# Latent attention on one NeuronCore: the low half of a split as a subtraction on VectorE, with a batch's side work in another order

## The chip, the cores and the metric

The kernel runs on one core of a Trainium2 chip. The metric is the device time of one execution in microseconds (us). Below, PE is TensorE's matmul, PEld its weight load, DVE is VectorE, ACT is ScalarE, POOL is GpSimd, and SP is SyncE, which issues most DMAs. L362 means line 362 of the kernel.

## The reference, cut to what matters

The input is 8 batches of 1024 tokens of width 256, all float32. A first stage is latent attention with 16 heads of 16 and one rotary part of 32 shared by all heads; a second stage is two layers of windowed attention with an MLP. The change is in the first stage only:

```python
xn = layernorm(x)
c_kv = xn @ W_kv_down                     # 256 -> 128
k_rope = rotary(c_kv @ W_k_rope);  q_rope = rotary(xn @ W_q_rope)
k = c_kv @ W_k_up;  v = c_kv @ W_v_up;  q = xn @ W_q      # 16 heads of 16
scores = (q . k per head + q_rope . k_rope) / sqrt(16 + 32), causal
x = x + softmax(scores) @ v @ W_o
...                                       # then two layers of the second stage
```

## The kernel before, in words

**Units and steps.** In `mla` the scores of a batch are cut into 36 units, each one a set of key blocks and queries that fills 512 columns for four heads. The loop `for step in range(len(units) ...)` runs one unit a step, 36 steps a batch, 8 batches, and then an epilogue that finishes the last units. The order of the instructions on PE, DVE, ACT and POOL is the written order (`manual_schedule`). A step s does, in this order:

- `scores` of unit s: 16-head products of `k` and `q` on PE (L461) into two tiles of two PSUM banks each, and two exponentials on ACT, 128x1024 each, into `pt` (L469). `pt` has six buffers, that is three units.
- `turned` of unit s-1: each of the two `pt` tiles is multiplied on DVE by `er`, the exponential of the rotary scores (L483). After the first of the two, `settle` runs what is owed on DVE from the step before (the output's add L576, and the rotary factors L342 and L349).
- `values` of unit s-2: products of `pt` and `v` on PE into `acc` (L496). When a group of heads is complete, `ended` copies `acc` on ACT.
- the side work that the table lists for the step, first what is not named `low`, then `low`.
- what has come due after `ended`: `inverse` three steps later (a reciprocal on DVE, L528, and the DMAs through `zr` that spread it; for the last pair of a batch also the verdict on the sums, L1846, L1847, L1840), and `scaled` seven steps later (a multiplication on DVE, L562).

**Side work.** The table before the loop holds (step, who, name, arguments). `who` is the batch relative to the one whose scores run: -1 is the batch before, 1 the next, 2 the one after it. Each batch needs all of this once:

- `load`, `statistics` (DVE), `normalise` (ACT), `turn` (four transposes on PE, a copy on ACT): x, normalised and transposed, as `xnT`.
- `down`, `value`, `rope_q`, `rope_k`: products on PE (all through `times`, L201, as four column tiles side by side), with a copy on ACT or a multiplication on DVE.
- `query` m, n, c: half c of the product for the q of eight heads and 512 tokens; `keys` m, n: the product for k. With the last half `halves` copies the sum from PSUM to `t[:, 0]` on ACT, rounded to the type float32r.
- `low`: the rest, sum minus rounded sum, which makes `t[:, 1]`. Before, PE adds the product of `minus` (minus the identity) and `t[:, 0]` onto the sum in PSUM (L362), and ACT copies the result. Then `place_q` or `place_k` issues two DMAs on SP that lay both halves out for `scores`. There are eight of these a batch.
- `rotary` c, kb: rotary scores of a key block on PE, 512 columns or fewer at the diagonal, and their exponential into `er` on ACT (L424), at the diagonal also a mask on POOL.
- `squares` (ACT) and `reach` (PE, and a maximum on DVE, L443): a check on the size of the rotary vectors.
- `out_add` t, i: half i of an output product on PE; after the second an add on DVE (L576) and a store to DRAM.

All single-bank products share a pool of two PSUM banks: a bank is free again when its last reader is through. For the batches before the first, the same table runs ahead of the loop (who 1 and 2 only). In the last batch, from the step `ALONE` on, which is one past the last step with who 0, the two banks become a third tile for `scores`. The second stage's first weights and tables are loaded when the memory of the first stage's side work is free, near the end of the last batch.

Of the kernel before, what the change touches and what calls it, by code (L numbers as in the profile page):

```python
# [30 lines left out]
F32R = mybir.dt.float32r  # L31
AF = mybir.ActivationFunctionType
ALU = mybir.AluOpType
# [3 lines left out]
P = 128  # L37
# [45 lines left out]
def preln_mla_local_kernel(  # L83
# [27 lines left out]
    nc = tc.nc  # L111
    B = x.shape[0]
# [4 lines left out]
    ident = const.tile([P, P], F32, name="ident")  # L117
# [38 lines left out]
    def mla(ctx: ExitStack, verdict):  # L156


        wp = ctx.enter_context(tc.tile_pool(name="w_mla", bufs=1))
# [23 lines left out]
        on_v, on_a = Evacuate(nc, "v"), Evacuate(nc, "a")  # L183
# [55 lines left out]
                    lo = (a if same else 1 - a) * HR  # L239
                    nc.scalar.copy(dst[:, :, n * DR + a * HR : n * DR + a * HR + HR], src[:, :, lo : lo + HR])  # L240

        minus = wp.tile([P, P], F32R, name="minus")
        nc.scalar.mul(minus, ident, -1.0)

        vs = []
        for i in range(2):
            t = of[i].tile([P, NT, NH * VW + 32 - VW], F32, name=f"v{i}")
# [15 lines left out]
        def settle():  # L263
            while owed:
                owed.pop(0)()

        class Batch:
# [91 lines left out]

            def low(self):  # L360
                ps, t, then, args = self.pending
                nc.tensor.matmul(ps, minus, t[:, 0], start=False, stop=True, skip_group_check=True)  # L362
                on_a(t[:, 1], ps)
                then(t.bitcast(F32), *args)

            def query(self, m, n, c, part=None):
# [218 lines left out]
        def at(step, who, name, *args):  # L585
            beside.setdefault(step, []).append((who, name, args))

        for step, who, *what in (
            (0, -1, "out_add", 4, 0), (0, 0, "query", 1, 1, 0), (0, 0, "squares", 0),
            (1, -1, "out_add", 4, 1), (1, 0, "query", 1, 1, 1),  # L590
            (2, -1, "out_add", 6, 0), (2, 0, "low"),
            (3, -1, "out_add", 6, 1), (3, 0, "squares", 1),
            (4, 0, "value", 2), (4, 0, "rotary", 1, 3),
            (5, 0, "rotary", 1, 4), (5, 0, "rotary", 1, 5),
            (6, 0, "rotary", 1, 6), (6, 0, "reach"),
            (7, 0, "rotary", 0, 0),
            (8, 0, "keys", 1, 0), (8, 1, "normalise", 0, 0),
            (9, 0, "query", 0, 0, 0), (9, 0, "low"),
            (10, 0, "query", 0, 0, 1),
            (11, 0, "low"), (11, 1, "normalise", 0, 1), (11, 1, "normalise", 0, 2), (11, 1, "statistics", 1, 0),  # L600
            (12, 0, "query", 1, 0, 0), (12, 0, "query", 1, 0, 1), (12, 1, "normalise", 0, 3),
            (13, -1, "out_add", 0, 0), (13, 0, "low"), (13, 1, "statistics", 1, 1),
            (14, -1, "out_add", 0, 1), (14, 0, "keys", 1, 1),
            (15, -1, "out_add", 2, 0), (15, 0, "low"),
            (16, -1, "out_add", 2, 1), (16, 1, "normalise", 1, 0), (16, 1, "normalise", 1, 1),
            (17, 0, "rotary", 0, 2), (17, 1, "turn", 0, 0),
            (18, 1, "turn", 0, 1),
            (19, 1, "down", 0, 0), (19, 1, "normalise", 1, 2),
            (20, 1, "down", 0, 1), (20, 2, "load"), (20, 1, "normalise", 1, 3),
            (21, 1, "turn", 1, 0), (21, 1, "turn", 1, 1),  # L610
            (22, 1, "keys", 0, 0),
            (23, 0, "rotary", 0, 1), (23, 1, "low"),
            (24, 1, "down", 1, 0), (24, 0, "rotary", 0, 3),
            (25, 1, "down", 1, 1),
            (26, 1, "value", 0), (26, 2, "statistics", 0, 0),
            (27, 1, "rope_k", 0), (27, 1, "value", 1),
            (28, 1, "rope_q", 0, 0), (28, 1, "rope_q", 0, 1),
            (29, 1, "query", 0, 1, 0), (29, 1, "query", 0, 1, 1),
            (30, 1, "low"),
            (31, 1, "value", 3), (31, 2, "statistics", 0, 1),  # L620
            (32, 1, "rope_q", 1, 0), (32, 1, "rope_q", 1, 1), (32, 1, "keys", 0, 1),
            (33, 1, "rope_k", 1), (33, 1, "low"),
            (34, 1, "rotary", 1, 0), (34, 1, "rotary", 1, 1),
            (35, 1, "rotary", 1, 2), (35, 1, "rotary", 1, 7),
        ):
            at(step, who, *what)

# [2 lines left out]
        def do(b, step, low=False):  # L630
            for who, name, args in beside.get(step, []):
                if (name == "low") == low and 0 <= b + who < B:
                    act = getattr(batches[b + who], name)

                    if b == B - 1 and who == 0 and name.startswith("out"):
                        held.append((act, args))
                    else:
                        act(*args)


        units = []
# [15 lines left out]
        line, due = [], []  # L657
        with tc.manual_schedule(engines={E.PE, E.DVE, E.Activation, E.Pool}):
            for b in range(B + 1):
                for step in range(len(units) if b < B else 17):  # L660
                    if b == B - 1 and step == ALONE:
                        banks.close()
                        third = banks.enter_context(tc.tile_pool(name="pscore2", bufs=1, space=PSUM))
                        shared = itertools.cycle((pscore, pscore, third))
                    if b < B:
                        if step == 0:
                            batches[b].start()
                        line.append((batches[b], units[step], batches[b].scores(step, units[step])))
                    if len(line) > 1 or b == B:
                        for bt, unit, pts in line[-2 : -1] if b < B else line[-1:] if step == 0 else []:  # L670
                            bt.turned(unit, pts)
                    if b == B and step == 0:
                        for act, args in held[:2]:
                            act(*args)
                    ended = []
                    if len(line) > 2 or b == B and line:
                        bt, unit, pts = line.pop(0)
                        ended = [(bt, e) for e in bt.values(unit, pts)]
                    if b == B and step == 0:
                        for act, args in held[2:]:  # L680
                            act(*args)
                    if b == B:
                        settle()
                    do(b, step)
                    do(b, step, low=True)
                    if b == B:
                        settle()
                    for what in due:
                        what[0] -= 1
                    while due and due[0][0] == 0:  # L690
                        due.pop(0)[1]()
                    for bt, (c, g) in ended:
                        if (bt.b, c) == (B - 1, 0):
                            bt.straight(g)
                        elif g % 2:
                            due.append([3, lambda bt=bt, c=c, g=g: bt.inverse(c, g // 2)])
                            due.append([7, lambda bt=bt, c=c, g=g: bt.scaled(c, g // 2)])
                            due.sort(key=lambda what: what[0])
# [1152 lines left out]
    with ExitStack() as one:  # L1851
        mla(one, verdict)
# [9 lines left out]
    with tc.tile_pool(name="psum_v", bufs=1, space=PSUM) as psum:  # L1862
        ps = psum.tile([1, 1], F32, name="psbad")
# [80 lines left out]
```

## Time and profile before

| what | us |
|---|---|
| median of 3 runs (lowest to highest) | 3214.92 (3214.23 to 3216.42) |
| the profiled execution | 3218.66 |
| its span, first to last instruction | 3216.7 |
| DVE L483, two a unit, x576 | 678.7 busy, 1221 ns each |
| ACT L469, two a unit, x576 | 559.3 busy, 1028 ns each |
| PE L496 and L461, x3072 each | 314.9 and 252.7 busy |

Busy time is the union of an engine's instructions; the mean of one is longer than the distance between two that are queued, since they overlap. Matmuls are pipelined and their ends are modelled, so PE's busy share says little alone. An answer on waits lists who waited for whom, the total, the times and the longest. The mean granted TensorE clock is 0.992 of full speed, and it is 1.00 in every middle batch of the first stage.

### The profile page before, as it was taken

To read this page: it belongs to the slowest core of one execution; us is meant where nothing else is said; L and a number is where in the kernel's file an instruction comes from. 1 tells how busy PE (TensorE), PEld (TensorE's weight loads), DVE (VectorE), ACT (ScalarE), POOL (GpSimd) and SP (SyncE) were. 2 spreads that over 40 slices of the span, in tenths; PEclk is the share of its full clock that TensorE was granted. 3 is DMA by queue.
4 is the path that set the end of the run, shared out by engine and by line. 5 is a ranking of instruction groups with operands and counts; after the bars stand their busy time and mean duration, and the time that the engine had idled before them with its cause. 6 is when DMAs were issued, how large, how long until landed. Compare 5 with 4: busy or idle time off the path is not lost.

```text
span 3216.7 us, 112643 instructions
## 1 busy us (share of the span) xinstructions
PE 3139.2 (98%) x50082; PEld 1453.9 (45%) x50082; DVE 2589.3 (80%) x3784; ACT 1738.6 (54%) x2179; POOL 1359.5 (42%) x1065
## 2 busy tenths in 40 slices
PE   8999999999877999999999999999999999999998
PEld 2443444444323444444445444444544445454454
DVE  5898989898869888787888877787877788787773
ACT  6999899988722444444444443444444443444441
POOL 1111110110047655555565554655555555554540
PEclk9999999999998999999999999999999999999999
DMA  4334333423444354454545445454544545454431
GB/s 120 82 88 116 74 99 91 119 70 85 121 128 116 92 145 113 126 132 109 130 120 146 115 121 159 113 146 133 149 125 126 138 123 135 134 149 117 119 108 55
DMA packets 411613, 376.99 MB, mean 117 GB/s; under 512 B 174655, under 2 KB 353262, under 8 KB 410990
## 3 DMA queue, kind: packets, MB, share of 16 engines
q1 hardware_dynamic: 409134, 367.29, 43.2%
q8 instruction: 395, 6.47, 0.9%
q10 hardware_dynamic: 1984, 2.41, 0.2%
q14 instruction: 100, 0.82, 0.1%
HBM read 173.82 MB, written 141.00 MB: 98 GB/s over the span
## 4 chain that ended last, share of the span: by engine, by line
PE 90%; DVE 3%; DMA 2%; ACT 1%; issue 1%; SPq 1%; POOL 0%; DVEq 0%; ACTq 0%; POOLq 0%
PE ag L722 19%; PE pair L722 13%; PE psy L722 10%; PE acc L496 8%; PE psw L722 7%; PE sc L461 6%; PE pv L722 6%; PE o L1055 6%; PE pair L1014 5%; PE psR L201 2%; PE psq L201 2%; PE s L1063 2%; PE psx L201 2%; ACT pt L469 1%; PE psc L201 1%
## 5 line engine op out<-in xcount | busy, mean ns | idle before, releaser
L483 DVE TENSOR_TENSOR pt<-pt,er 128x1024 f32<-128x1024 f32 x576 | 678.7, 1221 | 62.9 <-ACT pt L469 62.5
L958 POOL TENSOR_TENSOR t<-t,t 128x1024 f32<-128x1024 f32 x128 | 304.4, 2378 | 801.9 <-DVE t L954 801.9
L722 PE MATMUL ag<-d,l 128*32 128x512 f32 x5632 | 639.7, 593 | 1.2 <-DVE xs L1095 0.6
L469 ACT ACTIVATE pt<-sc 128x1024 f32<-128x1024 f32 x576 | 559.3, 1028 | 54.7 <-PE sc L461 39.3
L1020 ACT ACTIVATE pt<-pair 128x1024 f32<-128x1024 f32 (+1 forms) x256 | 235.2, 968 | 538.1 <-PE pair L1014 503.2
L722 PE MATMUL pair<-l_qkv,xT 128*32 128x512 f32 x4096 | 474.0, 599 | 3.8 <-DMA xT<-zx 2.6
L126 POOL TENSOR_TENSOR rn<-ss,half 128x16 f32<-128x16 f32 x128 | 373.2, 2916 | 13.7
L722 PEld LDWEIGHTS ag<-d,l 128*32 128x32 f32 x5632 | 177.6, 110 | 373.6 <-issue 354.9
L496 PE MATMUL acc<-pt,v 128*32 128x512 f32 (+3 forms) x3072 | 314.9, 496 | 10.4 <-DVE pt L483 10.2
L949 ACT ACTIVATE sq<-pair 128x1024 f32<-128x1024 f32 x128 | 131.2, 1025 | 350.4 <-issue 311.4
L722 PE MATMUL psy<-l,hid 128*32 128x256 f32 x5120 | 282.1, 379 | 0.0
L426 POOL TENSOR_SCALAR_AFFINE_SELECT er<-er 128x128 f32<-128x128 f32 x64 | 49.1, 771 | 532.0 <-ACT er L424 532.0
L722 PEld LDWEIGHTS pair<-l_qkv,xT 128*32 128x32 f32 x4096 | 132.0, 111 | 306.6 <-issue 284.0
L461 PE MATMUL sc<-q,k 32*128 32x512 f32 (+3 forms) x3072 | 252.7, 381 | 7.5 <-ACT pt L469 6.6
L951 DVE TENSOR_TENSOR t<-pair,l_cos 128x1024 f32<-128x1024 f32 x128 | 156.1, 1219 | 121.3 <-ACT sq L949 121.1
L964 POOL TENSOR_TENSOR t<-t,rn 128x1024 f32<-128x1024 f32 x128 | 243.7, 1904 | 10.0
L722 PE MATMUL pv<-l_qkv,xT 128*32 128x512 f32 x2048 | 247.3, 592 | 0.0
L1055 PEld LDWEIGHTS o<-pt,v 128*32 128x32 f32 x7680 | 215.3, 110 | 68.0 <-issue 51.9
L1187 DVE SCALAR_TENSOR_TENSOR hid<-ag,l_b,ge 128x512 f32<-128x512 f32 x160 | 116.8, 730 | 157.7 <-ACT ge L1186 86.5
L1055 PE MATMUL o<-pt,v 128*32 128x128 f32 x7680 | 234.8, 273 | 3.1 <-POOL pt L1022 2.8
L722 PE MATMUL psw<-l_o,oT 128*32 128x256 f32 x4096 | 237.0, 383 | 0.4 <-DVE xs L1224 0.4
L1073 DVE RECIPROCAL rs<-s 128x256 f32<-128x256 f32 x128 | 223.2, 1743 | 15.6 <-PE s L1063 15.5
(331 smaller groups left out, 4480.2 us busy)
## 6 DMA issues: line engine op xcount, KB each, us to landing
z<-turned SPq DMA_DIRECT2D x512, 128.0 KB
qkT<-z SPq DMA_DIRECT2D x128, 512.0 KB
y<-xs SPq DMA_DIRECT2D x128, 128.0 KB
h<-y SPq DMA_DIRECT2D x32, 512.0 KB
zx<-turneds SPq DMA_DIRECT2D x120, 128.0 KB
xT<-zx SPq DMA_DIRECT2D x240, 64.0 KB
zh<-turnedh SPq DMA_DIRECT2D x120, 128.0 KB
d<-zh SPq DMA_DIRECT2D x30, 512.0 KB
```

The lines of the kernel that those rows point to most:

```text
L126: nc.gpsimd.tensor_tensor(out_, in_, half[:, :n], ALU.pow)
L201: nc.tensor.matmul(out[four], w[:, four], rhs, start=start, stop=stop)
L461: nc.tensor.matmul(two[n // 2][:, n % 2, lo : lo + w], k[rows], q[rows, h], start=(h == 1), stop=(h == 0),)
L469: nc.scalar.activation(pt, sc, AF.Exp, scale=SCALE)
L483: nc.vector.tensor_tensor(t, t, er.to_broadcast([P, 1024 // w, w]), ALU.mult)
L496: nc.tensor.matmul(self.acc[g][32 * n : 32 * n + 32, q0 - c * 512 :], self.v[:, kb, h * VW - at : h * VW - at + 32], pts[n // 2][:, n % 2, ...
L722: nc.tensor.matmul(out[four], w[:, four], rhs, start=start, stop=stop)
L958: nc.gpsimd.tensor_tensor(t1, t1, t2, ALU.add)
L964: nc.gpsimd.tensor_tensor(t1, t1, rn.unsqueeze(3).to_broadcast([P, 2, HEADS, DH]), ALU.mult)
L1020: nc.scalar.activation(pt[:, :, : n * P], flat[:, :, : n * P], AF.Exp, scale=-1.0)
L1055: nc.tensor.matmul(o[32 * j : 32 * j + 32, g, a, :], vs[m][:, h * DH + a * 32 : h * DH + a * 32 + 32], pts[m][g][:, place(j), off : off + ...
L1073: nc.vector.reciprocal(rs, s)
```

## The change

`minus` goes. `low` subtracts on DVE: the sum is read from PSUM, `t[:, 0]` from SBUF, and `t[:, 1]` is written. ACT no longer copies a second time. The table holds the same 74 entries in other steps, some for another batch (for example `query` 1 1 and `squares` 0 now run a batch ahead, and `value` 3 in place of `value` 2 is the one that runs late). The epilogue has 15 steps in place of 17, since the last `out_add` stands in step 14.

```diff
--- before.py
+++ after.py
@@ -239,9 +239,6 @@
                     lo = (a if same else 1 - a) * HR
                     nc.scalar.copy(dst[:, :, n * DR + a * HR : n * DR + a * HR + HR], src[:, :, lo : lo + HR])
 
-        minus = wp.tile([P, P], F32R, name="minus")
-        nc.scalar.mul(minus, ident, -1.0)
-
         vs = []
         for i in range(2):
             t = of[i].tile([P, NT, NH * VW + 32 - VW], F32, name=f"v{i}")
@@ -359,8 +356,7 @@
 
             def low(self):
                 ps, t, then, args = self.pending
-                nc.tensor.matmul(ps, minus, t[:, 0], start=False, stop=True, skip_group_check=True)
-                on_a(t[:, 1], ps)
+                nc.vector.tensor_tensor(t[:, 1], ps, t[:, 0], ALU.subtract)
                 then(t.bitcast(F32), *args)
 
             def query(self, m, n, c, part=None):
@@ -586,42 +582,44 @@
             beside.setdefault(step, []).append((who, name, args))
 
         for step, who, *what in (
-            (0, -1, "out_add", 4, 0), (0, 0, "query", 1, 1, 0), (0, 0, "squares", 0),
-            (1, -1, "out_add", 4, 1), (1, 0, "query", 1, 1, 1),
-            (2, -1, "out_add", 6, 0), (2, 0, "low"),
-            (3, -1, "out_add", 6, 1), (3, 0, "squares", 1),
-            (4, 0, "value", 2), (4, 0, "rotary", 1, 3),
-            (5, 0, "rotary", 1, 4), (5, 0, "rotary", 1, 5),
-            (6, 0, "rotary", 1, 6), (6, 0, "reach"),
-            (7, 0, "rotary", 0, 0),
-            (8, 0, "keys", 1, 0), (8, 1, "normalise", 0, 0),
-            (9, 0, "query", 0, 0, 0), (9, 0, "low"),
-            (10, 0, "query", 0, 0, 1),
-            (11, 0, "low"), (11, 1, "normalise", 0, 1), (11, 1, "normalise", 0, 2), (11, 1, "statistics", 1, 0),
-            (12, 0, "query", 1, 0, 0), (12, 0, "query", 1, 0, 1), (12, 1, "normalise", 0, 3),
-            (13, -1, "out_add", 0, 0), (13, 0, "low"), (13, 1, "statistics", 1, 1),
-            (14, -1, "out_add", 0, 1), (14, 0, "keys", 1, 1),
-            (15, -1, "out_add", 2, 0), (15, 0, "low"),
-            (16, -1, "out_add", 2, 1), (16, 1, "normalise", 1, 0), (16, 1, "normalise", 1, 1),
-            (17, 0, "rotary", 0, 2), (17, 1, "turn", 0, 0),
-            (18, 1, "turn", 0, 1),
-            (19, 1, "down", 0, 0), (19, 1, "normalise", 1, 2),
-            (20, 1, "down", 0, 1), (20, 2, "load"), (20, 1, "normalise", 1, 3),
-            (21, 1, "turn", 1, 0), (21, 1, "turn", 1, 1),
-            (22, 1, "keys", 0, 0),
-            (23, 0, "rotary", 0, 1), (23, 1, "low"),
-            (24, 1, "down", 1, 0), (24, 0, "rotary", 0, 3),
-            (25, 1, "down", 1, 1),
-            (26, 1, "value", 0), (26, 2, "statistics", 0, 0),
-            (27, 1, "rope_k", 0), (27, 1, "value", 1),
-            (28, 1, "rope_q", 0, 0), (28, 1, "rope_q", 0, 1),
-            (29, 1, "query", 0, 1, 0), (29, 1, "query", 0, 1, 1),
-            (30, 1, "low"),
-            (31, 1, "value", 3), (31, 2, "statistics", 0, 1),
-            (32, 1, "rope_q", 1, 0), (32, 1, "rope_q", 1, 1), (32, 1, "keys", 0, 1),
-            (33, 1, "rope_k", 1), (33, 1, "low"),
-            (34, 1, "rotary", 1, 0), (34, 1, "rotary", 1, 1),
-            (35, 1, "rotary", 1, 2), (35, 1, "rotary", 1, 7),
+            (0, 0, "value", 3),
+            (1, -1, "out_add", 6, 0), (1, 0, "keys", 1, 0),
+            (2, -1, "out_add", 6, 1), (2, 0, "low"), (2, 0, "squares", 1),
+            (3, 0, "rotary", 0, 0), (3, 0, "rotary", 1, 5), (3, 1, "statistics", 1, 0),
+            (4, 0, "rotary", 1, 4),
+            (5, 0, "rotary", 1, 3),
+            (6, 0, "reach"), (6, 1, "statistics", 1, 1),
+            (7, 0, "rotary", 1, 6), (7, 0, "rotary", 1, 7), (7, 1, "normalise", 0, 0),
+            (8, -1, "out_add", 4, 0), (8, -1, "out_add", 4, 1), (8, 1, "normalise", 0, 1),
+            (8, 1, "normalise", 0, 2), (8, 1, "normalise", 0, 3),
+            (9, 0, "query", 0, 0, 0), (9, 0, "query", 0, 0, 1),
+            (10, -1, "out_add", 0, 0), (10, -1, "out_add", 0, 1), (10, 0, "low"), (10, 1, "normalise", 1, 0),
+            (10, 1, "normalise", 1, 1),
+            (11, 0, "query", 1, 0, 0),
+            (12, 0, "query", 1, 0, 1),
+            (13, 1, "turn", 0, 0), (13, 0, "low"), (13, 1, "normalise", 1, 2),
+            (14, -1, "out_add", 2, 0), (14, -1, "out_add", 2, 1), (14, 1, "turn", 0, 1),
+            (15, 0, "keys", 1, 1),
+            (16, 1, "down", 0, 0), (16, 0, "low"), (16, 1, "normalise", 1, 3),
+            (17, 1, "down", 0, 1), (17, 1, "turn", 1, 0),
+            (18, 0, "rotary", 0, 2), (18, 1, "turn", 1, 1),
+            (19, 1, "query", 0, 1, 0),
+            (20, 1, "query", 0, 1, 1), (20, 2, "load"),
+            (21, 1, "down", 1, 0), (21, 1, "low"),
+            (22, 1, "down", 1, 1),
+            (23, 0, "rotary", 0, 1), (23, 0, "rotary", 0, 3),
+            (24, 1, "keys", 0, 0),
+            (25, 1, "value", 1), (25, 1, "low"), (25, 2, "statistics", 0, 0),
+            (26, 1, "rope_q", 0, 0),
+            (27, 1, "rope_q", 0, 1), (27, 1, "value", 0),
+            (28, 1, "rope_k", 0),
+            (29, 1, "keys", 0, 1), (29, 2, "statistics", 0, 1),
+            (30, 1, "rope_q", 1, 0), (30, 1, "rope_q", 1, 1), (30, 1, "low"),
+            (31, 1, "value", 2),
+            (32, 1, "rope_k", 1), (32, 1, "rotary", 1, 0),
+            (33, 1, "rotary", 1, 1), (33, 1, "squares", 0),
+            (34, 1, "query", 1, 1, 0), (34, 1, "query", 1, 1, 1),
+            (35, 1, "rotary", 1, 2), (35, 1, "low"),
         ):
             at(step, who, *what)
 
@@ -657,7 +655,7 @@
         line, due = [], []
         with tc.manual_schedule(engines={E.PE, E.DVE, E.Activation, E.Pool}):
             for b in range(B + 1):
-                for step in range(len(units) if b < B else 17):
+                for step in range(len(units) if b < B else 15):
                     if b == B - 1 and step == ALONE:
                         banks.close()
                         third = banks.enter_context(tc.tile_pool(name="pscore2", bufs=1, space=PSUM))
```

## The prediction

> **What bounds the kernel now.** I read the page first, then the busy time by batch of the attention stage, then the chain of waits and the list of waits in one of its batches, and at last single rows of the timeline. The change touches only the attention stage, which holds the first 901 us.
>
> ```profile
> PE 3139.2 (98%) x50082; PEld 1453.9 (45%) x50082; DVE 2589.3 (80%) x3784; ACT 1738.6 (54%) x2179; POOL 1359.5 (42%) x1065
> ```
>
> Over the whole span PE looks full, but a busy PE is modelled, so I count its work below. Cut at the first exponential of each batch, the columns being the length and then the busy time of PE, PEld, DVE, ACT and POOL:
>
> ```profile
> 41.34:146.40 105.06, 102.30 (x1109) 40.08 (x1112) 92.39 (x100) 96.07 (x127) 12.15 (x15) 1.00 0.30 71
> 470.61:578.50 107.89, 107.58 (x1268) 44.12 (x1272) 97.30 (x111) 97.67 (x129) 11.96 (x15) 1.00 0.38 95
> 794.22:901.50 107.28, 94.92 (x1045) 37.50 (x1045) 93.14 (x96) 83.54 (x99) 6.27 (x12) 0.97 0.44 116
> ```
>
> Six middle batches last 107.9 us each, the first 105.1, the last 107.3. DVE and ACT are both busy 90% of a middle batch. The chain and the waits in that batch:
>
> ```profile
> by line: PE acc L496 31.8%; PE sc L461 25.4%; PE psR L201 7.2%; PE psx L201 6.4%; PE psq L201 6.4%; PE psv L201 3.2%; PE psk L201 3.2%; PE psc L201 3.2%; PE psrq L201 3.2%; PE psn L204 2.0%; ACT pt L469 1.9%; issue 1.8%; PE psrk L201 1.6%;
> 507.49 1.72 PE psq L201 x16
> ```
> ```profile
> PEld sc L461 <- ACT pt L469: 13.4, 24, 0.8
> DVE pt L483 <- ACT pt L469: 7.4, 16, 1.0
> PEld acc L496 <- DVE pt L483: 4.0, 11, 0.4
> ```
>
> The chain runs through PE nearly all the way. DVE waits for ACT, that is, it is ahead; PE's waits for DVE are at most 0.4 us long.
>
> **A price list from rows.** Sixteen matmuls of 512 columns take 1.72 us in the chain, four side by side, so four cost 0.43. A step (one unit of 512 keys-by-queries columns) has 16 such matmuls: 1.71 us of PE. Beside it stands side work: a half of a query product, a keys product, a value, an output half, 0.85 each; a rotary block 0.21 to 0.85; a turn 0.43. Over the 36 steps that adds up to 104.2 us of 107.9: PE has 3.7 us of true slack. ACT needs 1.88 a step for two exponentials (0.94 apart when queued) and about 0.55 for a copy or a 512-wide exponential, 98.2 in all. A step with nothing beside it is not limited by PE's 1.71 but by ACT and PE in turn:
>
> ```profile
> 850.41 1.94 ACT L469 ACTIVATE pt<-sc 128x1024 f32<-128x1024 f32 x2 [0.60 <-PE sc L461]
> 852.97 1.94 ACT L469 ACTIVATE pt<-sc 128x1024 f32<-128x1024 f32 x2 [0.61 <-PE sc L461]
> ```
>
> That is 2.55 us. I price a step at the largest of PE's sum, 0.93 of ACT's sum (ACT-heavy steps borrow from neighbours) and 2.55. For the order of before this gives, in groups of six steps, 19.1, 17.2, 18.2, 16.0, 18.4 and 18.8: 107.6 against 107.9 measured. So the rule misses 0.3.
>
> **Part 1, the product and the eviction go.** Rows of both and of the nearest things to the new subtraction:
>
> ```profile
> 504.68 0.50 PE L362 MATMUL psq<-alves_place_q(0, 0)_6275,minus 128*128 128x512 f32 x1
> 505.11 0.44 PE L461 MATMUL sc<-q,k 32*128 32x384 f32 x2
> ```
> ```profile
> L79 ACT CAST alves_place_k(1, 1)_6461<-psk 128x512 fp32r<-128x512 f32 x2 | 1.2, 588 | 0.7 <-ACT odd L79 0.3 <-PE psk L362 0.3
> L342 DVE TENSOR_TENSOR rq<-psrq,tab 128x512 f32<-128x512 f32 x2 | 1.4, 692 | 0.6 <-PE psrq L201 0.6
> L576 DVE TENSOR_TENSOR x<-psx,x 128x512 f32<-128x512 f32 x4 | 2.7, 684 | 0.0
> ```
>
> The product with `minus` holds PE from 504.68 to 505.11: 0.43, and 8 a batch are 3.4 us off PE's 104.2, leaving 100.8. The second eviction goes from ACT: 8 x 0.55 = 4.4. The first stays, and the subtraction waits for it as the product did. No row shows a subtraction that writes the rounded type; two DVE rows with one input in PSUM and the same shape take 0.68 to 0.69, 0.60 to 0.62 when queued. I take 0.62, the same form but for the type (bounds: 0.35, as the 128x32 reciprocal at L528, and 1.15, as a 1024-wide L483, which would put 4.2 more a batch on DVE and lead to (b) or (c) below). DVE has 97.0 a batch by the prices below (97.3 busy), gains 8 x 0.62 = 5.0 and comes to 102.0. What is queued behind each subtraction is the next unit's pair of multiplications, and behind those PE's `values`.
>
> **Part 2, the order.** The set of side work is the same; only steps differ. The same rule gives 17.2, 18.2, 17.8, 15.4, 16.2 and 18.8: 103.6, or 103.9 with the 0.3. Parts 1 and 2 would so save 4.0 a batch, if DVE keeps up. The DMAs that move along on SP (each low half's two, the output's stores, the two z writes of an `inverse`) I cost at nothing: the tightest halves, those of `keys` 1 1, are stored in step 16 and read in step 21, some 13 us later, and were stored one step earlier before; were that cover gone, `scores` would wait for a transfer.
>
> It does not everywhere. DVE's work per step is 2.29 for two multiplications (1.145 apart when queued), 0.62 for an add, a scaling or a subtraction, 1.1 for two statistics, 0.64 for the reduction in `reach`. In groups of six DVE has, after, 17.8, 18.0, 15.9, 15.0, 17.8, 17.4, which is above the step times in the first and the fifth group (before: 16.8, 16.1, 16.5, 14.4, 16.0, 17.4). The worst run is steps 2 to 6. Step 3 gets an add, statistics and a scaling (4.6 us), step 4 an `inverse` with the verdict on its sums, step 6 `reach` and statistics (4.1). The verdict is seen here:
>
> ```profile
> 484.29 0.35 DVE L528 RECIPROCAL rs<-rs 128x32 f32<-128x32 f32 x1
> 484.67 0.23 DVE L1846 TENSOR_SCALAR oka<-rs 128x128 f32<-128x128 f32 x1
> ...
> 485.47 4.62 DVE L483 TENSOR_TENSOR pt<-pt,er 128x1024 f32<-128x1024 f32 x4
> ...
> 492.00 0.69 DVE L443 TENSOR_REDUCE norms<-reach 128x1 f32<-128x512 f32 x1 [1.91 <-PE reach L442]
> ```
>
> From 484.29 to 485.47, 1.18 us. Before, DVE has caught up by `reach` (it waits 1.91 there); after, its lag grows by 0.2, 1.4, 0.9, -0.3 and 1.5 in steps 2 to 6, to 3.8. How much lag is free, one unit shows (its exponentials, its multiplications, its `values`):
>
> ```profile
> 399.10 1.95 ACT L469 ACTIVATE pt<-sc 128x1024 f32<-128x1024 f32 x2
> 400.17 2.36 DVE L483 TENSOR_TENSOR pt<-pt,er 128x1024 f32<-128x1024 f32 x2 [0.19 <-ACT pt L469]
> 405.06 1.07 PE L496 MATMUL acc<-pt,v 128*32 128x384 f32 x16
> ```
>
> DVE is done at 402.53, PE reads at 405.06: 2.5 us, in which two steps took 6.07 (the second pair of exponentials after these starts at 405.17). With two steps of 2.6 it is 0.9 less, with two of 2.9 it is 2.3; I take 1.5 to 2.0. So PE waits 1.8 to 2.3 there, and up to 0.5 about steps 25 to 30, where a subtraction and statistics share step 25. I take 2.3 a batch (bounds 0 and 4). A middle batch is then 103.9 + 2.3 = 106.2, 1.7 less than now; six give 10.2.
>
> First batch: it has no output adds. The rule gives 105.0 before and 101.1 after; with 0.3 and about 1.0 of waits, 102.4: 2.7 less than the measured 105.1. Last batch: it has no work for a next one; steps 0 to 24 sum to 71.1 by the rule (72.2 measured) and to 68.4 after, 2.7 less, one step of this because the third score pool opens at step 24 and not 25 (step 25 takes 1.8). Its end waits for weight loads, ACT and DVE both held for some 6 us about 870 to 881; I let that stay. Prologue: `query` 1 1 moves ahead of the loop (1.7 of PE) and three low halves there get shorter (each by a PE product with 0.84 of idle before it); I take +1.0 (bounds -1.5 and +2). The two steps cut from the epilogue hold nothing.
>
> Sum: 10.2 + 2.7 + 2.7 - 1.0 = 14.6 us. The profiled execution took 3218.66, 1.96 around its span of 3216.7, and becomes 3204.1; it is 3.7 above the median of 3214.92, which becomes 3200.3.
>
> **Rivals.** (a) DVE's lag is absorbed by the six buffers of `pt`: no waits, 6 x 4.0 + 3.7 + 2.7 - 0.5 = 30, 3185. For it: at 846.96 eight multiplications run in one queue and no PE wait over 0.4 is seen. Against it: 3.8 us of lag is more than a step. (b) The waits eat it all: 4 a batch, and the first and last batch alone gain; 3210 to 3217. (c) Slower: DVE becomes the limit and keeps its present idle time, because each subtraction and `reach` ties it to the engine that is late. Busy 97.3 + 5.0, idle 10.6 as now, gives 112.9 a batch, 5.0 more over seven: 3250. It decides from the point where DVE keeps over 5.6 of its 10.6 us of idle. Against it: that idle is mostly time in which DVE was ahead of ACT (7.4 of it by the waits shown). That the edit does nothing, because the first eviction still stands on the path, is part of (b).
>
> The Trainium skill, page "Perfetto Trace Analysis", sections "Identifying the Most-Contended Engine" and "Optimizing Scalar/DVE Operations", says to judge Vector and Scalar by occupancy, TensorE not by matmul busy time, and to offload a saturated DVE to Scalar. By it DVE and ACT at 90% are the limit here, the move goes the wrong way, and the result is (c). The trace's chain, 94% on PE, speaks against it.
>
> **How the numbers follow.** My sum 0.50, (a) 0.18, (b) 0.15, (c) 0.17. The predicted time is my sum's, 3200; its own range by the prologue and waits of 1.3 to 3.3 is 3193 to 3208. The range of 3181 to 3219 takes in (a) and (b) with 4 us for the prologue and the loads at the end. About 0.2%, 6.4 us, is what can be told from no change: faster is below 3208.5, that is all of (a) and my sum but for its edge: 0.68. Same takes most of (b): 0.14. Slower 0.18.
>
> **What would show it.** Right: no L362 product; DVE busy near 102 in a middle batch of 105.5 to 107; PE's longest waits for L483 over 1 us, in steps 5 to 8; ACT near 93. Wrong: batches at 104 with no such waits (a), or above 108 with DVE idle before L483 (c).

## The result and the profile after

The changed kernel's median is 3205.15 us of nine runs (3199.87 to 3206.73); the kernel before, run between them, has 3214.92 (3212.26 to 3218.53). The ratio is 0.9967, with an interval of 0.9957 to 0.9977: faster, by 9.8 us of the medians. The profiled execution took 3205.15, its span is 3203.4. That is 13.3 us shorter than the profiled span before, 3216.7.

The page's line of engines:

```profile
PE 3125.8 (98%) x50018; PEld 1450.0 (45%) x50018; DVE 2623.0 (82%) x3848; ACT 1708.4 (53%) x2114; POOL 1370.3 (43%) x1065
```

PE and ACT lost 64 and 65 instructions (8 low halves in each of 8 batches, and the making of `minus`), DVE won 64. DVE is 33.7 us busier, ACT 30.2 less, PE 13.4 less.

Lines have moved: L483 is now L479 (multiplication), L469 L465 (exponential), L496 L492 (`values`), L461 L457 (`scores`), L443 L439 (the maximum in `reach`), L562 L558 (`scaled`), L531 L527 and L533 L529 (`zr` and `by`), L577 L573 (the store of the output); the load of `x` is L189 in both. The subtraction is L359. The windows from one batch's first exponential to the next, with the same columns as before (length, then busy PE, PEld, DVE, ACT, POOL):

```profile
40.38:142.46 102.08, 99.83 (x1097) 40.03 (x1096) 95.69 (x109) 92.50 (x119) 13.62 (x14) 1.00 0.31 74
142.46:248.60 106.14, 106.14 (x1258) 43.76 (x1256) 101.58 (x119) 94.01 (x120) 12.84 (x14) 1.00 0.39 97
568.37:677.18 108.81, 107.25 (x1258) 44.45 (x1256) 101.50 (x119) 94.06 (x121) 13.06 (x14) 1.00 0.37 95
783.32:888.40 105.08, 93.31 (x1034) 37.41 (x1032) 95.57 (x100) 79.30 (x93) 8.78 (x12) 0.95 0.45 118
```

The eight batches last 102.08, 106.14, 106.35, 106.37, 107.05, 108.80, 106.14 and 105.08; before they lasted 105.06, 107.85, 108.46, 107.89, 107.89, 107.86, 107.86 and 107.29. Two things are to be seen: a middle batch that nothing disturbs takes 106.14, and some batches take more with the same work. The attention stage ends at 888.40 in place of 901.5: 0.96 comes from the prologue, 2.98 from the first batch, 6.96 from the six middle ones, 2.21 from the last, 13.1 in all. The rest of the span is as long as before (2315.0 and 2315.2). In the profiled executions of all the kernels below, that rest, whose code no edit changes, takes between 2307.5 and 2315.2; so a few us between two whole times can come from there, and the end of the attention stage is the better measure.

In the undisturbed batch (142.46 to 248.60), the chain by line and the list of waits (who waits for whom: total, times, longest):

```profile
by line: PE acc L492 34.7%; PE sc L457 27.3%; PE psR L201 7.3%; PE psx L201 6.9%; PE psq L201 6.5%; PE psv L201 3.3%; PE psk L201 3.2%; PE psc L201 3.2%; PE psrq L201 3.2%; PE psn L204 2.2%; PE psrk L201 1.6%; PE reach L438 0.8%
```
```profile
PEld sc L457 <- ACT pt L465: 18.2, 24, 0.8
ACT pt L465 <- PE sc L457: 7.9, 12, 1.5
PEld acc L492 <- DVE pt L479: 5.9, 15, 0.8
DVE pt L479 <- ACT pt L465: 3.4, 8, 0.7
DVE oT L558 <- DMA by<-zr: 0.9, 1, 0.9
```

The chain is all PE now; `minus` is gone from it, and ACT with it. DVE waited 7.4 us for exponentials before and waits 3.4 now, PE waited 4.0 for DVE and waits 5.9: DVE has lost about half of its lead by these waits. The subtraction by form in that batch:

```profile
L359 DVE TENSOR_TENSOR alves_place_k(1, 1)_2315<-psk,alves_place_k(1, 1)_2315 128x512 fp32r<-128x512 f32 x1 | 0.7, 684 | 0.0
```

684 ns here, 680 to 692 over the eight.

In the batch of 108.8 (568.37 to 677.18), three waits are longer than in the undisturbed batch or new:

```profile
PEld acc L492 <- DVE pt L479: 8.2, 16, 1.7
DVE oT L558 <- DMA by<-zr: 3.6, 1, 3.6
PE acc L492 <- DVE pt L479: 1.5, 1, 1.5
```

DVE waits 3.6 for a transfer (0.9 in the undisturbed batch), and PE then for DVE: 1.7 and 1.5 at the longest, where it was 0.8. The prediction has no such wait.

### The profile page after: what moved, and what is told of

Its sections match the earlier page's. It is cut to its first block, busy times and chain, and to the rows that moved or that the text cites. A ratio compares the mean times of both kernels' runs of the same rounds, so it can differ in the third digit from the quotient of the medians.

```text
span 3203.4 us, 112567 instructions
## 1 busy us (share of the span) xinstructions
PE 3125.8 (98%) x50018; PEld 1450.0 (45%) x50018; DVE 2623.0 (82%) x3848; ACT 1708.4 (53%) x2114; POOL 1370.3 (43%) x1065
## 4 chain that ended last, share of the span: by engine, by line
PE 90%; DVE 4%; DMA 3%; ACT 1%; SPq 1%; issue 1%; POOL 0%; ACTq 0%; DVEq 0%
PE ag L720 18%; PE pair L720 13%; PE psy L720 10%; PE acc L492 8%; PE psw L720 7%; PE sc L457 6%; PE pv L720 6%; PE o L1053 6%; PE pair L1012 5%; PE psR L201 2%; PE psx L201 2%; PE psq L201 2%; PE s L1061 2%; DVE pt L479 1%; PE psv L201 1%; PE psc L201 1%
## 5 line engine op out<-in xcount | busy, mean ns | idle before, releaser
L479 DVE TENSOR_TENSOR pt<-pt,er 128x1024 f32<-128x1024 f32 x576 | 676.3, 1220 | 31.8 <-ACT pt L465 31.2
L465 ACT ACTIVATE pt<-sc 128x1024 f32<-128x1024 f32 x576 | 559.2, 1027 | 86.2 <-PE sc L457 70.3
L492 PE MATMUL acc<-pt,v 128*32 128x512 f32 (+3 forms) x3072 | 326.3, 498 | 5.3 <-DVE pt L479 5.0
L422 POOL TENSOR_SCALAR_AFFINE_SELECT er<-er 128x128 f32<-128x128 f32 x64 | 59.7, 942 | 583.8 <-ACT er L420 583.0
L457 PE MATMUL sc<-q,k 32*128 32x512 f32 (+3 forms) x3072 | 257.1, 382 | 11.2 <-ACT pt L465 11.0
L457 PEld LDWEIGHTS sc<-q,k 32*128 32x128 f32 x3072 | 145.2, 184 | 209.6 <-ACT pt L465 161.5
```

The lines of the kernel that those rows point to most:

```text
L457: nc.tensor.matmul(two[n // 2][:, n % 2, lo : lo + w], k[rows], q[rows, h], start=(h == 1), stop=(h == 0),)
L465: nc.scalar.activation(pt, sc, AF.Exp, scale=SCALE)
L479: nc.vector.tensor_tensor(t, t, er.to_broadcast([P, 1024 // w, w]), ALU.mult)
L492: nc.tensor.matmul(self.acc[g][32 * n : 32 * n + 32, q0 - c * 512 :], self.v[:, kb, h * VW - at : h * VW - at + 32], pts[n // 2][:, n % 2, ...
```

## The experiments

All ratios are to the kernel before, run on the same chip in the same comparison, with their 95% intervals. "Middle batches" are the second to the seventh, each from its first exponential to the next batch's; a step is timed from the first exponential of its unit to that of the next.

**Each half of the change alone.** First the subtraction in the old order (the two lines of `minus` go, the table stays):

```diff
-                nc.tensor.matmul(ps, minus, t[:, 0], start=False, stop=True, skip_group_check=True)
-                on_a(t[:, 1], ps)
+                nc.vector.tensor_tensor(t[:, 1], ps, t[:, 0], ALU.subtract)
```

> The order of before with the subtraction alone (part 1 without part 2). My theory: taking 3.4 us a batch off PE is worth something in any order. The step rule gives 104.7 + 0.3 for this order, and DVE's lag reaches 2.0 to 2.4 us in five steps, so about 0.7 of waits: 105.7 a batch, 2.2 less than before, some 3200 in all. Rival 1, the order makes the gain and the subtraction only moves a wait from ACT to DVE: 107.5 to 108 a batch, 3212 to 3217. Rival 2, DVE at 102 us is the limit by its sum: 106 or more a batch, as after.

Then the new table with the product and its eviction, the same edit the other way round:

> The order of after with the product and the eviction of before (part 2 without part 1). My theory: PE is back at 104.2, the step rule gives 107.2 + 0.3, and DVE's lag in steps 3 to 8 (up to 3.5 us without a subtraction) costs about 1.5: 109 a batch, some 3222, or 3215 if that lag is free here because the steps are longer. Rival 1, the order makes the gain: 106 a batch, 3203 to 3207.

Measured: the subtraction alone gives 0.9987 [0.9978, 0.9996], 3209.87 beside 3213.91, and the new order alone 1.0013 [1.0004, 1.0022], 3218.93, which is slower. A middle batch of each, the subtraction alone first:

```profile
143.38:250.53 107.15, 105.84 (x1260) 42.98 (x1264) 101.11 (x119) 93.70 (x120) 16.30 (x15) 1.00 0.38 96
```
```profile
148.93:257.42 108.49, 108.49 (x1268) 45.09 (x1269) 97.69 (x111) 97.97 (x129) 14.21 (x14) 1.00 0.37 95
```

The end of the attention stage is at 901.5 before, at 893.8 with the subtraction alone, at 906.05 with the order alone and at 888.40 with both: -7.7, +4.5, -13.1. So the order is worth 5.4 on top of the subtraction, and costs 4.5 without it. With the product back, PE has its 104.2 again, and the new order has longer steps where it stands beside other work: step 10 takes 3.88, step 13 3.73 and step 30 3.90, with the subtraction 3.45, 3.27 and 3.48. The idea that the order alone makes the gain is out. My own figure for the subtraction alone, 105.7 a batch, is missed as well: the middle batches are 106.8 to 108.0. By step, those with a low half in 2, 11, 15 and 33 take 0.3 to 0.5 less than before and step 13 0.2 less; 9 and 30, which hold one too, take the same, and 12 and 14 take 0.5 and 0.2 more. That leaves 1.0 a batch, and step 23, where DVE waits for `by` (11.9 us in five waits, 3.8 before), gives up to 1.2 of it back. Why steps 12 and 14 grow stays open.

**What DVE's work costs.** The subtraction twice, into the same place:

```diff
                 nc.vector.tensor_tensor(t[:, 1], ps, t[:, 0], ALU.subtract)
+                nc.vector.tensor_tensor(t[:, 1], ps, t[:, 0], ALU.subtract)
```

> After, with each subtraction issued twice: 5.0 us more a batch on DVE and nothing else. My theory, PE's waits come from DVE's lag in a few steps, with lag made up elsewhere: the lag beyond 1.5 to 2.0 us grows by 2.5 a batch, to 108.6, some 3222 in all. Rival 2, DVE is the limit by its sum: each us counts, 111 a batch, some 3240. Rival 3, DVE's lag is free: 3205.

0.9987 [0.9977, 0.9996], 3209.40. The undisturbed batch:

```profile
144.46:251.99 107.53, 107.53 (x1258) 44.70 (x1256) 106.39 (x127) 93.97 (x120) 13.12 (x14) 1.00 0.38 96
```

4.8 us more of DVE cost 1.39 us a batch. It is neither the 5.0 of a DVE that sets the pace, nor the 2.5 that I expected, nor nothing. DVE is now busy in 99% of the batch, with 0.6 us of waits left; I take it that only here its sum begins to count.

The other direction: the low half off DVE, made on POOL instead.

```diff
-                nc.vector.tensor_tensor(t[:, 1], ps, t[:, 0], ALU.subtract)
+                nc.gpsimd.tensor_tensor(t[:, 1], t[:, 0], t[:, 0], ALU.subtract)
```

> After, with the low half written by POOL as the rounded half minus itself, so the low half of q and k is left out (zero) and DVE does nothing for it. My theory: the part of the waits that subtractions cause goes; DVE's lag in steps 3 to 6 is still there without the subtraction of step 2 (the lag then peaks at 3.6 and not 3.8), but steps 8 to 10 and 25 to 30 get free: 105.0 to 105.5 a batch, 3197 to 3201. Rival 2, DVE is the limit by its sum: its 97 us lie below PE's, and a batch takes 103.9: 3190. Rival 3, lag is free: 3205.

0.9962 [0.9948, 0.9975], 3200.88, and the undisturbed batch still takes 106.14, not the 105.0 to 105.5 that I expected (others take up to 108.8, with 11.8 us of waits for `by`). But it does not settle the question, for DVE got little freer: 100.03 busy in place of 101.58, though eight subtractions of 0.69 are gone.

```profile
141.93:248.07 106.14, 106.14 (x1258) 43.97 (x1256) 100.03 (x111) 94.02 (x121) 27.99 (x22) 1.00 0.38 97
```

The multiplication over the whole run (shortest/median/longest in ns), here and then in the changed kernel:

```profile
L479 DVE TENSOR_TENSOR pt<-pt,er x576: 1155/1218/2060, 40.9 to 891.8; 128x1024 f32<-128x1024 f32 x192
```
```profile
L479 DVE TENSOR_TENSOR pt<-pt,er x576: 1156/1218/1316, 41.4 to 890.8; 128x1024 f32<-128x1024 f32 x192
```

A multiplication of two SBUF tiles takes up to 2060 ns beside POOL's subtraction, and never over 1316 without it; each of the 45 that are longer than 1316 overlaps such a subtraction. The edit gave back in contention more than half of what it took away: without any work for the low half, as in the next run, DVE's busy time in this batch falls by 3.85, here by 1.55. The Trainium skill, page "SBUF — State Buffer", section "Who interferes with whom", says that a DVE instruction with two SBUF inputs contends with a GpSimd instruction that reads SBUF; these rows agree.

So the low half was taken off every engine: two tiles are allotted once with their second halves zeroed, and `halves` uses them in turn.

```diff
-                t = p1.tile([P, 2, 512], F32R, tag="halves", ...)
+                t = halves[next(turns) % 2]
...
-                nc.vector.tensor_tensor(t[:, 1], ps, t[:, 0], ALU.subtract)
```

> After without any work for the low half: the two buffers of halves are allotted once, their low parts are set to zero in the prologue, and `low` only issues its two DMAs. The low half of q and k is left out, and no engine does anything in its place (with POOL in its place DVE got only 1.5 us shorter, since its multiplications took up to 2.06 us beside POOL). DVE falls to 97. Theory A, what counts is where DVE's work lies: step 6 still has its statistics behind `reach` and step 8 its 4.3 us: 105.8 to 106.1 a batch, 3197 to 3200. Theory B, DVE's sum counts: 104 a batch, 3188 to 3190.

0.9957 [0.9940, 0.9973], 3198.75. All six middle batches take 106.1 to 106.17:

```profile
141.80:247.97 106.17, 106.17 (x1258) 43.77 (x1256) 97.73 (x111) 93.99 (x121) 13.12 (x14) 1.00 0.39 97
```

3.9 us less of DVE, and the batch is as long as with the subtractions. Inside an undisturbed batch the subtractions cost nothing, and DVE's sum is not what makes 106.14 out of 103.6.

**The place of the wait.** Where PE exceeds the rule of the prediction is found by step: step 6 takes 2.95 to 2.98 in the six middle batches (the rule says 2.56) and step 8 4.32 to 4.35 (3.42). DVE from step 2 on:

```profile
149.66 1.23 DVE L479 TENSOR_TENSOR pt<-pt,er 128x1024 f32<-128x1024 f32 x1 [0.37 <-ACT pt L465]
...
152.54 0.75 DVE L283 BATCH_NORM_STATS2 bnst<-x 128x6 f32<-128x256 f32 x2
153.20 0.30 DVE L285 BATCH_NORM_AGGREGATE mv<-bnst 128x2 f32<-128x6 f32 x2
153.50 0.69 DVE L558 TENSOR_TENSOR oT<-oT,by 128x512 f32<-128x512 f32 x1
...
157.79 4.62 DVE L479 TENSOR_TENSOR pt<-pt,er 128x1024 f32<-128x1024 f32 x4
...
162.33 0.68 DVE L439 TENSOR_REDUCE norms<-reach 128x1 f32<-128x512 f32 x1
162.93 0.74 DVE L283 BATCH_NORM_STATS2 bnst<-x 128x6 f32<-128x256 f32 x2
163.59 0.30 DVE L285 BATCH_NORM_AGGREGATE mv<-bnst 128x2 f32<-128x6 f32 x2
163.93 0.17 DVE L289 TENSOR_SCALAR ve<-mv 128x4 f32<-128x4 f32 x1
164.00 4.62 DVE L479 TENSOR_TENSOR pt<-pt,er 128x1024 f32<-128x1024 f32 x4
```

And PE:

```profile
165.49 1.54 PE L492 MATMUL acc<-pt,v 128*32 128x512 f32 x6
166.41 0.11 PEld L492 LDWEIGHTS acc<-pt,v 128*32 128x32 f32 x2 [0.77 <-DVE pt L479]
```

At 149.66 DVE waits for an exponential for the last time; from there to 180.52 its timeline shows no wait. So it is behind, and its lag is the sum of what the prediction listed for steps 3 to 6: statistics, a scaling, the verdict, `reach` and statistics again. The subtraction of step 2 runs at 148.6, ahead of that wait, and adds nothing to it. At 162.33 the four multiplications are through, and the maximum of `reach` and then 1.07 us of statistics of the next batch come ahead of unit 6's multiplications, which so start at 164.00. PE's `values` wait 0.77 for one of those at 166.41. This order is the same without subtractions: counted from the batch's first exponential, the maximum, the statistics and the multiplications start at +19.87, +20.47 and +21.54 here, and at +19.88, +20.48 and +21.55 where the low halves are left out. Moving the two pairs of statistics alone should then take the wait away:

```diff
-            (3, 1, "statistics", 1, 0),
-            (6, 1, "statistics", 1, 1),
+            (1, 1, "statistics", 1, 0),
+            (8, 1, "statistics", 1, 1),
```

> After, with the second half's statistics in steps 1 and 8, where DVE has room, and not in 3 and 6. Theory A: step 8 takes 4.33 us where the step rule says 3.42, and step 6 2.96 where it says 2.56, because DVE, which must wait for `reach` on PE in step 6, then does 1.1 us of statistics before the multiplications of unit 6, and is already late from step 3: both excesses go, 1.2 a batch, 104.9, some 3196 to 3198. Theory B: step 8 is long because of three normalisations on ACT beside two output halves on PE: it stays at 4.3, and the time at 3204 to 3206.

0.9939 [0.9925, 0.9952], 3193.28. DVE has the same sum, and the batch is 1.38 shorter:

```profile
142.57:247.33 104.76, 104.76 (x1258) 43.59 (x1256) 101.30 (x119) 93.87 (x120) 13.14 (x14) 1.00 0.39 98
```

DVE at the same place:

```profile
161.84 0.69 DVE L439 TENSOR_REDUCE norms<-reach 128x1 f32<-128x512 f32 x1 [0.33 <-PE reach L438]
162.44 4.71 DVE L479 TENSOR_TENSOR pt<-pt,er 128x1024 f32<-128x1024 f32 x4
```

Now DVE is early: it waits 0.33 for PE's `reach`, and unit 6 starts 1.67 sooner after the batch's first exponential (+19.87 for +21.54). Of the 1.67, 1.07 is the pair behind `reach`; 0.60 is the maximum, which starts that much sooner (+19.27 for +19.87) without the pair of step 3. Step 6 takes 2.55 and step 8 3.41, what the rule says. Both pairs moved in one edit, so what each is worth alone is not shown.

**The late transfer.** In the batch of 108.8 the queue of SP reads so:

```profile
619.52 0.51 SPq L573 DMA_DIRECT2D x2d<-x  x1
623.78 0.39 SPq L189 DMA_DIRECT2D x<-in_L_attn_x_dram  x1
624.22 1.25 SPq L387 DMA_DIRECT2D k<-alves_place_k(1, 1)_7867  x2
625.51 0.98 SPq L189 DMA_DIRECT2D x<-in_L_attn_x_dram  x1
626.59 1.55 SPq L527 DMA_DIRECT2D zr<-rs  x2
631.55 0.62 SPq L529 DMA_DIRECT2D by<-zr  x1
```

and DVE at its end:

```profile
636.03 0.69 DVE L558 TENSOR_TENSOR oT<-oT,by 128x512 f32<-128x512 f32 x1 [3.60 <-DMA by<-zr]
```

In the chain of waits the pieces between are `x2d<-x` for 4.24, `zr<-rs` for 3.90 and `by<-zr` for 4.36. The load of a later batch's `x` (L189) needs the buffer that the store of `x2d` still reads, so it stands 4.3 us at the head of SP; `zr` and `by`, which have nothing to do with it, stand behind. In the four other batches with a load it is ahead of `zr` too, but it starts 2.5 to 2.6 after the store; `by` is issued 10.3 to 10.5 after the store, and DVE waits for it up to 1.8. Before, in the batch from 362.72, `zr` was issued at 415.96, ahead of that load at 419.45, and `by` 5.2 after the store. The load is ahead of `zr` in both kernels with the new table (the order alone too), behind it in both with the old one; SP is not among the engines whose order `manual_schedule` fixes. Two kernels test it. One asks for `scaled` a step later:

```diff
-    due.append([7, lambda bt=bt, c=c, g=g: bt.scaled(c, g // 2)])
+    due.append([8, lambda bt=bt, c=c, g=g: bt.scaled(c, g // 2)])
```

> After, with `scaled` due eight steps after the end of a group and not seven. Theory A: what makes after's batches differ (106.1 to 108.8) is DVE waiting in `scaled` for the DMA that fills `by`, up to 3.6 us at once, which then holds PE at step 23; a step more of time takes the wait away: all middle batches at 106.1 to 106.4, 3201 to 3203, and less spread between runs. Theory B: the wait at step 23 has another cause and the DMA's lateness only shows there: 3205, batches still uneven.

The other lets POOL issue the loads of `x` after the first batch:

```diff
-                nc.sync.dma_start(
+                (nc.gpsimd if b else nc.sync).dma_start(
```

> After, with the loads of x of batches 1 to 7 issued by POOL and not by SP, where they stand ahead of the `zr` writes and wait for the store of the batch before. Theory A (SP's queue makes `by` late): the wait at step 23 goes, 3201 to 3203. Theory B (the DMAs themselves are slow, not the queue): as after, 3205, with waits of DVE for `by` as before.

With `scaled` a step later: 0.9950 [0.9936, 0.9963], 3196.52, middle batches 105.97 to 106.12, and 0.8 us of DVE's waits for `by` left of 7.4. With POOL's loads: 0.9964 [0.9950, 0.9977], 3199.76, all middle batches 106.12 to 106.14, and no wait for `by` at all. SP in that run:

```profile
619.34 0.52 SPq L573 DMA_DIRECT2D x2d<-x  x1
621.66 1.80 SPq L527 DMA_DIRECT2D zr<-rs  x2
625.11 0.63 SPq L529 DMA_DIRECT2D by<-zr  x1
```

`by` is issued 5.8 after the store in place of 12.0. So the load ahead of `zr` is the cause. What POOL's loads win they half lose again: the first exponential comes at 42.15 in place of 40.38; why the prologue is longer with them stays open.

Here the subtractions do cost something. Where the low halves are left out, the load is still ahead of `zr`, but the store before it goes out 49.1 to 49.8 us into the batch in place of 50.6 to 51.4, and DVE has no wait for `by`: from the first exponential the stage takes 843.5 in place of 848.0.

**Both together.** The spread statistics with POOL's loads:

> Both edits, the spread statistics and the loads on POOL. If both theories A hold and the gains add: 1.2 a batch and some 3 in all, 3192 to 3195. If the two hide each other, 3197.

0.9934 [0.9921, 0.9948], 3192.75: middle batches of 104.8, but the first exponential at 42.23. The spread statistics with `scaled` a step later, beside the changed kernel again:

> Spread statistics and `scaled` a step later, loads on SP as in after. If the two waits are apart and both gains add: all middle batches 104.8 and no wait for `by`, the prologue as in after: the last exponentials end at 876 to 877 us and the time is some 3189 to 3191, 2 to 3 below the version with the loads on POOL. If the later `scaled` brings DVE's lag to a worse step: 105.5 and more.

> After as it is, beside the next one on the same chip. Both theories: the ratio to before of the first comparison, 0.996 to 0.998, with middle batches of 106.1 and some of them 0.2 to 2.7 longer at step 23.

The changed kernel again gives 0.9955 [0.9942, 0.9969], 3199.30; with both edits it is 0.9928 [0.9914, 0.9942], 3189.48, the fastest that does all the work and 9.8 us below the changed kernel beside it. Its batch:

```profile
141.26:246.10 104.84, 104.84 (x1258) 43.57 (x1256) 100.84 (x119) 93.93 (x120) 14.35 (x14) 1.00 0.39 98
```

Last, that kernel with the low halves left out, to see whether DVE holds what is left above 103.6:

> The same taken from the version with spread statistics and `scaled` a step later. Theory A: 104.8 a batch as with the subtractions, since nothing waits for DVE there any more; what is left over the step rule's 103.6 is the rule's own error in steps with one product and one copy. Theory B: 103.6 to 104, 3182 to 3184.

0.9925 [0.9909, 0.9942], 3188.15; middle batches of 104.76 to 104.81.

```profile
140.72:245.51 104.79, 104.79 (x1258) 43.57 (x1256) 97.18 (x111) 93.93 (x120) 14.72 (x14) 1.00 0.39 98
```

It does not: 3.7 us less of DVE change nothing here either.

## Why the prediction was right, and where it was not

The time, 3205 against 3200 in a range of 3181 to 3219, and the sign came out; the sum came out as 13.5 in the profiled execution (3218.66 to 3205.15) against 14.6. Between medians it is 9.8 in the first comparison and 14.4 in the second (3213.65 to 3199.30). By the end of the attention stage, 888.40 and 887.75 in the two profiled executions of the changed kernel, it is 13.1 and 13.8; the rest of the span takes 2315.0 in the one and 2309.7 in the other.

- **The work that leaves PE** was sized rightly. By itself it gives 7.7 by the end of the attention stage, and only with it the new order gains, 5.4 more. No L362 is left, ACT is at 94.01 for about 93, DVE at 101.58 for 102.0, the subtraction takes 0.68 to 0.69 by itself. An undisturbed middle batch takes 106.14 for 106.2.
- **"So PE waits 1.8 to 2.3 there"** is right in its place (steps 2 to 8) and in its mechanism: DVE runs without a wait through the work that was named for steps 3 to 6, and PE waits for it in steps 6 to 8. The size is wrong. It costs 0.4 in step 6 and 0.9 in step 8, 1.38 as measured by moving the statistics. The subtractions are no part of it: without any the batch is as long (106.17). So the sign that I named, waits of over 1 us for the multiplication, did not show; the longest in an undisturbed batch is 0.8.
- **"103.6, or 103.9 with the 0.3"** was too low by about as much as the wait was too high. Without the wait the batch is 104.76, whatever DVE has to do (104.79 without low halves). Steps with one product and one copy beside the unit take 2.6 to 2.73 where the rule says 2.56. The two errors, 0.9 and 0.9, cancel: 106.2 is right partly by luck.
- **"Up to 0.5 about steps 25 to 30"**: nothing was lost there.
- **"The DMAs that move along on SP ... I cost at nothing"** failed. I counted the z writes among them, but worked out a cover only for the low half of `keys` 1 1. What was late was `zr`, behind a load that the table does not even move (step 20 in both). The middle batches' excess over 106.14 is 4.0 us in the profiled run (0.21 + 0.23 + 0.91 + 2.66), and 3.6 of it lies in step 23 of the three batches with the longer waits for `by` (0.10, 0.86 and 2.61); the other 0.4, in steps 23 and 27, has no such wait beside it. From the first exponential the stage takes 848.0, and 843.4 with `scaled` a step later. So the late transfer is about what the six batches miss, 6.96 for 10.2; 0.8 came back, since before they took 0.4 more in all than six times 107.9, and an undisturbed one takes 106.14 in place of 106.2. In the second run of the changed kernel the excess is 2.3, with 5.7 us of waits for `by`.
- **The prologue** was put at +1.0 and measured -1.0 (first exponential at 41.34 before, 40.38 after), within the bounds. Each half does what I named: the shorter low halves give 2.5 (38.86 with the subtraction alone), the order costs 2.4 (43.74 with it alone). Together they give 0.1 and not the 1.0 that was measured, so the size stays unexplained.
- **First and last batch** gave 3.0 and 2.2 for 2.7 each.
- **Rival (a)**, no waits at all, is out for this kernel, as its condition fails in step 8; had the statistics stood elsewhere it would have been near, with batches of 104.8 for its 103.9. **Rival (b)** is out: the six batches gained. **Rival (c)** is out, and with it what the occupancy rule of the Trainium skill ("Perfetto Trace Analysis", "Identifying the Most-Contended Engine") gave here: DVE is 96% busy in a batch, the highest of the engines whose busy time is not modelled, and the time fell; taking 3.9 us from it gives nothing, and only at 99% does adding 4.8 cost 1.4. Its idle time was mostly a lead over ACT and was used up, as the waits had suggested.

What stays open: why the subtraction alone, in the old order, loses again in steps 12 and 14 and so gives 107.1 in place of 105.7; what each pair of statistics is worth; and why the load starts 4.3 us after the store in one batch and 2.5 in the others, which makes `by` so late there.

## What to carry to other kernels

A product that only subtracts, and its eviction, can become one subtraction from PSUM when PE's columns are what fill the batch and the engine that takes it over has a lead. What matters is not that engine's sum over the batch but what stands in its queue over a stretch in which it cannot catch up, ahead of the tiles that PE reads: moving two pairs of statistics, 1.0 and 1.1 us, out of it was worth 1.4 a batch, removing 3.9 us of subtractions nothing inside it. Read every in-order queue again after the order of work changes, the DMA queue too: a load that waits for its buffer holds up small transfers behind it that are needed sooner.

## What the runs showed of the hardware

A DVE multiplication of two float32 tiles in SBUF (128x1024) grows from 1218 ns to as much as 2060 ns beside a POOL subtraction that reads SBUF. POOL's own rows there are 1033 to 2107 ns, of an operation of half that width (128x512). In the middle batches the granted clock stays 1.00 through all of PE's waits.
